# Moving part of the last image's feed-forward evictions from ScalarE to VectorE in a convolution, scan and attention kernel

## The chip, the cores and the metric

The kernel runs on one core of one Trainium2 chip. The metric is the device time of one execution in microseconds (us), of which the median of several runs is taken.

The core has five engines with a queue of their own each. PE (TensorE) multiplies matrices into PSUM, DVE (VectorE) and ACT (ScalarE) work element by element and read PSUM and SBUF, POOL (GpSimd) works element by element on SBUF, and SP (SyncE) issues the transfers (DMAs) between SBUF and the device's main memory. An engine takes its instructions in the order in which the program issued them. Where one needs another engine's result, it waits on a semaphore.

## What is computed

Eight images of 96 channels and 64 x 64 points go through two layers. Layer 0 is a normalization, a projection with a depthwise convolution, a selective scan in four directions, and two further convolutions with a channel gate. Layer 1 is a linear attention (no softmax) and a feed-forward net whose products take e5m2 operands and whose sums are rounded to float16. The part that matters here is the feed-forward net:

```python
q_mul = lambda x: _float_quantize(x, 5, 2)     # e5m2
q_acc = lambda x: _float_quantize(x, 5, 10)    # float16
def _qlinear(x, W, b):
    y = q_acc(jnp.einsum('bsk,nk->bsn', q_mul(x), q_mul(W)))
    return q_acc(y + q_mul(b))
h = jax.nn.relu(_qlinear(x, W1, b1))           # 96 -> 384
y = _qlinear(h, W2, b2)                        # 384 -> 96
...
t = t + _L1_attn_ref(_ln_t(t), ...)
t = t + _L1_ffn_ref(_ln_t(t), ...)
```

So the inner layer's sum is rounded to float16, a bias is added, the result is cut at zero and rounded to float16 again, and then it is rounded to e5m2 as the operand of the second product.

## The kernel before

Data lie with channels on the partitions. The 4096 points of an image are cut into 8 chunks of 512 (`T`), and nearly every instruction works on one chunk. The work of an image has three parts: `front` (normalization, projection, convolution), the scan (the long loop over `units`, line 1092 on), and `back_end` (gate, two convolutions, attention, feed-forward). While the scan of one image runs, the front of the next image and the back end of the one before are issued between the scan's instructions, a step at a time. Only the back end of the last image has no scan to lie beside.

That last back end is issued behind the scan, from line 1152 on. Four sets of tiles, called kits, take the chunks in turn: `kit_b` with the tag f1, and three more with the tags f0, y01 and y2. `side_by_side` runs one stage after the other, and in each stage one stream for each kit. With 8 chunks and 4 kits, each kit does 2 chunks of a stage, so a stage has two rounds. The stages are `first_conv`, `second_conv`, `channel_gate`, `attention`, `joined` and `feed_forward`, the last.

A stream is a Python generator. `drained` (and `tick`) advance a clock by one, and let each stream whose time is due issue its next step, kit after kit: f1, f0, y01, y2. A `yield n` asks to be called again n ticks later. The clock exists only while the program is written: it sets the order of the instructions in each engine's queue, and no time on the chip. With all four streams at the same step, each engine's queue has step k of f1, f0, y01 and y2, and then step k + 1 of the four.

`bank(k.tag, ...)` gives a kit its PSUM bank. For the tags f0, f1, y01 and y2 there is one bank each (`BANKS`), so that a kit's next product can be written only when its last has been read out.

One chunk of `feed_forward` is, by lines:

- 767 to 769: PE multiplies the normalized tokens by the attention's matrix, and DVE adds bias and residue (`scalar_tensor_tensor`) into `t`.
- 773, through `norm` (376 to 384) and `inv_std` (369, 370): PE centres, ACT squares and copies, PE averages the squares, and ACT makes the inverse deviation with Ln and Exp.
- 774: DVE multiplies and writes `x8` in e5m2.
- 776 to 782: for each third `f` of the inner layer, PE multiplies (778), and ACT reads the sum out into the float16 tile `h16` (780) and then adds bias and applies Relu in place (781).
- 783: ACT rounds the whole of `h16`, 128 x 1536, to e5m2 in `h8`.
- 787: PE makes the second product in three matmuls.
- 789, 790: ACT reads it out into `o16` and adds the bias.
- 792: POOL adds it to `t`, and 793 asks for the transfer to the output.

A request that goes through `later` is issued 3 ticks on (`HOLD`). The tokens of the second round are asked for at line 771, in the first round.

Of the kernel before, what the change touches and what calls it, by code (L numbers as in the profile page):

```python
# [12 lines left out]
AF = mybir.ActivationFunctionType  # L13
ALU = mybir.AluOpType
# [29 lines left out]
def kernel(ctx: ExitStack, tc: tile.TileContext, a, out):  # L44
# [8 lines left out]
    nc = tc.nc  # L53
# [9 lines left out]
    def bank(tag, name):  # L63
        return psum.tile([P, T], F32, tag=tag, name=name, bufs=BANKS[tag])
# [48 lines left out]
    def later(dst, src):  # L113

        requests.append((clock[0] + HOLD, dst, src))

    def tick():
        clock[0] += 1
        while requests and requests[0][0] <= clock[0]:
            _, dst, src = requests.pop(0)  # L120
            nc.sync.dma_start(dst, src)  # L121
# [60 lines left out]
    with tc.tile_pool(name="raw", bufs=1) as rp:  # L182
# [10 lines left out]
        def widened(name, shape):  # L193
            t = wp.tile(shape, F32, name=name)
            nc.vector.tensor_copy(t, quantized(name, shape, rp))
            return t
# [3 lines left out]
        b1, b2 = widened("b1", [P, 3]), widened("b2", [C, 1])  # L200
# [81 lines left out]
    def landed(*parts):  # L282
        while clock[0] < max(p.ready for p in parts):
            yield 1
# [25 lines left out]
    def back_kit(pool, tag, extra, other=None, upper=0):  # L310

        k = Kit()
        k.tag, k.solo, k.upper = tag, not extra, upper
        if other is None:
            k.ya, k.za, k.bs, k.r, k.d1, k.s1, k.s2, y, z = (plain(pool, f"{tag}b{i}") for i in range(9))
            k.pad = padded(pool, tag + "pad")
        else:
            k.ya, k.za = (x.t for x in other.x)
            k.bs, k.r, k.d1, k.s1 = other.e
            k.s2, y, z = (other.pre[:, i, :] for i in range(3))  # L320
            k.pad = other.pad
        k.yb, k.zb = Part(y), Part(z[64:P])
        k.ya, k.za, k.bs = Part(k.ya), Part(k.za), Part(k.bs)
        if pool is None:
            return k
        k.t2 = Part(k.r), k.ya
        k.ln = Part(pool.tile([C + 1, T], F32, name=tag + "ln"))
        nc.gpsimd.memset(k.ln.t, 1.0)
        k.im = other.im if other else Part(pool.tile([C + 1, 18, W2], F32, name=tag + "im"))
        k.m3 = [Part(pool.tile([C, 8, W2], F32, name=f"{tag}m3{i}")) for i in range(2)]  # L330
        k.gm = gm0 if not extra else pool.tile([P, 8, W2], F32, name=tag + "gm")
        if extra:
            nc.gpsimd.memset(k.gm, 0.0)
        k.x8 = pool.tile([C, T], F8, name=tag + "x8")
        k.h16 = pool.tile([P, 3, T], F16, name=tag + "h16")
        k.h8 = pool.tile([P, 3, T], F8, name=tag + "h8")
        k.o16 = pool.tile([C, T], F16, name=tag + "o16")
        return k
# [33 lines left out]
    def norm(k, srcs, sq, d):  # L372

        ps = bank(k.tag, "ctr")[:C, :]
        for i, src in enumerate(srcs):
            nc.tensor.matmul(ps, cen_c, src, start=i == 0, stop=i == len(srcs) - 1)  # L376
        yield PA
        nc.scalar.activation(sq, ps, AF.Square)
        nc.scalar.copy(d, ps)  # L379
        yield 1  # L380
        ps = bank(k.tag, "var")[:C, :]
        nc.tensor.matmul(ps, ones_c, sq, start=True, stop=True)  # L382
        yield PA
        inv_std(ps, ps)
        yield 1
        return ps

    place = [None]
    CALM = (0, 1, 8, 9, 16, 17)

# [136 lines left out]
    def back_end(b, s):  # L527
# [212 lines left out]
        def normed_again(k, n, c):  # L740
            fetch(k.ln, lnd[:, bass.ts(c, T)])
            fetch(k.t2[n % 2], x1d[:, bass.ts(c, T)])
# [18 lines left out]
        def feed_forward(k, cs):  # L761

            for n, c in enumerate(cs):
                t = k.t2[n % 2].t[:C]
                yield from landed(k.ln, k.t2[n % 2])
                ps = bank(k.tag, "att")[:C, :]
                nc.tensor.matmul(ps, small["qkvf"], k.ln.t, start=True, stop=True)
                yield PA
                nc.vector.scalar_tensor_tensor(t, ps, bff, t, ALU.add, ALU.add)  # L769
                if n + 1 < len(cs):  # L770
                    normed_again(k, n + 1, cs[n + 1])
                yield 1
                rs = yield from norm(k, (t,), k.s1[:C], k.d1[:C])
                nc.vector.tensor_tensor(k.x8, k.d1[:C], rs, ALU.mult, saturate=False)
                yield 1
                for f in range(3):
                    ps = bank(k.tag, "ff1")
                    nc.tensor.matmul(ps, w1[:, bass.ts(f, P)], k.x8, start=True, stop=True)
                    yield PA
                    nc.scalar.copy(k.h16[:, f, :], ps)  # L780
                    nc.scalar.activation(k.h16[:, f, :], k.h16[:, f, :], AF.Relu, bias=b1[:, f : f + 1])
                    yield 1
                nc.scalar.activation(k.h8, k.h16, AF.Copy, saturate=False)
                yield 1
                ps = bank(k.tag, "ff2")[:C, :]
                for f in range(3):
                    nc.tensor.matmul(ps, w2[:, f, :], k.h8[:, f, :], start=f == 0, stop=f == 2)
                yield PA
                nc.scalar.copy(k.o16, ps)
                nc.scalar.activation(k.o16, k.o16, AF.Identity, bias=b2)  # L790
                yield 2
                nc.gpsimd.tensor_tensor(t, t, k.o16, ALU.add)  # L792
                later(out[b, :, bass.ts(c, T)], t)
                yield 1

        chunks = range(NC)[::-1]
        return (
            (gated, chunks), (first_conv, chunks[1::2]), (second_conv, chunks), (channel_gate, None),
            (attention, chunks), (joined, None), (feed_forward, chunks),
        )  # L800


    def settled():

        yield SETTLE
# [19 lines left out]
    def drained(*streams):  # L825
        while any(s.on for s in streams):
            tick()
            for s in streams:
                s.run()

    def all_issued():
        drained(Stream(iter((HOLD + 1,))))

    def side_by_side(stages, kits):

        for stage, cs in stages:
            todo = [cs] if cs is None else [cs[i :: len(kits)] for i in range(len(kits))]
            drained(*(Stream(stage(k, c)) for k, c in zip(kits, todo)))
            drained(Stream(settled()))
# [312 lines left out]
    with tc.tile_pool(name="end", bufs=1) as pool:  # L1152
        kits = [kit_b, back_kit(pool, "f0", True, kit_f, 1)]
        kits += [back_kit(pool, t, True, None, i) for i, t in enumerate(("y01", "y2"))]
        drained(Stream(settled()))
        side_by_side(final[1:], kits)
        all_issued()

# [66 lines left out]
```

## Time and profile before

| what | us |
|---|---|
| median of 3 runs | 11342.24 |
| lowest and highest of the 3 | 11338.22, 11354.75 |
| the profiled execution's own time | 11372.37 |
| its span in the trace | 11370.7 |
| first ACT instruction of the last `feed_forward`, from the span's start | 11297.59 |
| last DMA of the output issued | 11367.74 |

The profile is that of one execution. Times in the trace count from the span's start. A line of the timeline gives start, duration, engine, line, operation, output and inputs by the program's names, shapes, and in brackets the idle time of the engine ahead of it and what ended it. The names are cut: `f1h`, `f0h`, `y01h` and `y2h` stand for both `h16` and `h8` of the four kits, `f1o` for `o16`, `f1x` for `x8`, `ff` for the PSUM banks. A row of the list of groups gives line, engine, operation, names, shapes and count, then the busy time in us and the mean of one in ns, and then the idle time ahead of it. The table by stretches gives for each engine the busy time in the stretch and, in brackets, the number of instructions.

### The profile page before, as it was taken

To read this page: it belongs to the slowest core of one execution; us is meant where nothing else is said; L and a number is where in the kernel's file an instruction comes from. 1 tells how busy PE (TensorE), PEld (TensorE's weight loads), DVE (VectorE), ACT (ScalarE), POOL (GpSimd) and SP (SyncE) were. 2 spreads that over 40 slices of the span, in tenths; PEclk is the share of its full clock that TensorE was granted. 3 is DMA by queue.
4 is the path that set the end of the run, shared out by engine and by line. 5 is a ranking of instruction groups with operands and counts; after the bars stand their busy time and mean duration, and the time that the engine had idled before them with its cause. 6 is when DMAs were issued, how large, how long until landed. Compare 5 with 4: busy or idle time off the path is not lost. (4 is left out here: it accounts for less than half of the span.)

```text
span 11370.7 us, 97041 instructions
## 1 busy us (share of the span) xinstructions
PE 8567.3 (75%) x23270; PEld 2328.5 (20%) x23270; DVE 10367.4 (91%) x10828; ACT 7508.4 (66%) x14939; POOL 10398.7 (91%) x2783
## 2 busy tenths in 40 slices
PE   6577657887778877888678876788768887676677
PEld 2111112222122211222112221222212221111122
DVE  0799999999999999999999999999999999999991
ACT  3566656767666676667766676666766667666674
POOL 0799999999999999999999999999999999999990
PEclk8678778888788877889778887888878888787787
DMA  2788878898888888888888888889888888888872
GB/s 71 171 197 197 201 189 210 209 225 196 203 210 212 219 198 202 210 215 215 195 207 210 216 214 194 210 205 228 202 200 211 212 220 195 198 198 195 201 188 78
DMA packets 1081039, 2253.24 MB, mean 198 GB/s; under 512 B 419609, under 2 KB 420314, under 8 KB 949395
## 3 DMA queue, kind: packets, MB, share of 16 engines
q1 hardware_dynamic: 1080467, 2247.05, 81.3%
q8 instruction: 184, 3.01, 0.1%
q14 instruction: 388, 3.18, 0.1%
HBM read 1507.14 MB, written 336.69 MB: 162 GB/s over the span
## 5 line engine op out<-in xcount | busy, mean ns | idle before, releaser
L946 POOL TENSOR_TENSOR hb<-b,du 128x2048 f32<-128x2048 f32 x1536 | 6939.0, 4535 | 21.3 <-DMA du<-ua 14.3
L1062 ACT ACTIVATE da<-delta,w_a_logs 128x512 f32<-128x512 f32 x6144 | 4216.7, 689 | 696.3 <-DVE hb L1123 575.8
L972 PE MATMUL p<-hb,halves 128*64 128x512 f32 x12288 | 3822.7, 731 | 800.1 <-POOL hb L952 382.1
L1123 DVE TENSOR_TENSOR_SCAN da<-da,carry,hb 128x512 f32<-128x512 f32 x3087 | 3949.0, 1279 | 58.0 <-ACT da L1062 54.3
L952 POOL TENSOR_TENSOR hb<-hb,c 128x2048 f32<-128x2048 f32 (+2 forms) x768 | 2984.9, 3887 | 304.7 <-ACT carry L1131 252.2
L1123 DVE TENSOR_TENSOR_SCAN hb<-da,carry,hb 128x512 f32<-128x512 f32 x2289 | 2781.0, 1264 | 57.7 <-ACT da L1062 56.7
L1125 DVE TENSOR_TENSOR hb<-da,c 128x512 f32<-128x512 f32 x3528 | 2440.5, 692 | 154.0 <-DVE da L1123 0.9
L1126 ACT COPY carry<-da 128x1 f32<-128x1 f32 x3528 | 554.9, 157 | 2351.6 <-DVE hb L1125 2341.1
L972 PEld LDWEIGHTS p<-hb,halves 128*64 128x64 f32 x12288 | 916.2, 161 | 3540.7 <-issue 2129.5
L434 PE MATMUL conv<-f0im,taps 97*128 97x512 f32 (+1 forms) x2088 | 903.5, 664 | 95.9 <-ACT f0pre L490 54.3
L928 POOL TENSOR_TENSOR ua<-nat,ua 128x512 f32<-128x512 f32 x256 | 327.3, 1279 | 257.5 <-DMA b<-xd 257.5
L1123 DVE TENSOR_TENSOR_SCAN da<-da,hb 128x512 f32<-128x512 f32 x441 | 537.7, 1219 | 26.0 <-POOL hb L946 24.6
L925 DVE SCALAR_TENSOR_TENSOR nat<-dt,nat 128x512 f32<-128x512 f32 x384 | 259.5, 676 | 238.9 <-ACT nat L923 238.9
L911 PE MATMUL dt<-dts,dt_w 7*64 7x512 f32 (+1 forms) x1024 | 450.0, 657 | 16.9 <-DVE nat L925 12.4
L981 PE MATMUL p<-u,ident 128*128 128x512 f32 x768 | 438.3, 699 | 3.6 <-DMA u<-y 3.6
L376 PE MATMUL ctr<-f1b,cen_c 96*96 96x512 f32 x460 | 271.9, 697 | 193.4 <-DVE f1b L769 158.8
L434 PEld LDWEIGHTS conv<-f0im,taps 97*128 97x128 f32 (+1 forms) x2088 | 254.6, 174 | 681.6 <-issue 523.5
L1123 DVE TENSOR_TENSOR_SCAN hb<-da,hb 128x512 f32<-128x512 f32 x327 | 377.9, 1204 | 4.9 <-ACT da L1062 4.9
L382 PE MATMUL var<-f1b,ones_c 96*96 96x512 f32 x346 | 207.4, 684 | 153.6 <-ACT f1b L379 145.3
L792 POOL TENSOR_TENSOR f1b<-f1b,f1o 96x512 f32<-96x512 f32 x58 | 67.7, 1167 | 252.0 <-ACT f1o L790 251.9
L1131 ACT COPY carry<-hb 128x4 f32<-128x4 f32 (+2 forms) x768 | 146.8, 191 | 197.4 <-DVE hb L1123 184.8
L655 PE MATMUL cab<-f1m,cab_w 96*96 96x512 f32 x348 | 206.0, 719 | 90.9 <-ACT f1b L664 41.4
(416 smaller groups left out, 7710.5 us busy)
## 6 DMA issues: line engine op xcount, KB each, us to landing
b<-xd SPq DMA_DIRECT2D x1024, 512.0 KB
c<-xd SPq DMA_DIRECT2D x1024, 512.0 KB
delta<-nat SPq DMA_DIRECT2D x1536, 128.0 KB
du<-ua SPq DMA_DIRECT2D x1024, 128.0 KB
y<-yt SPq DMA_DIRECT2D x512, 256.0 KB
u<-y SPq DMA_DIRECT2D x384, 256.0 KB
ua<-u SPq DMA_DIRECT2D x256, 256.0 KB
du<-ub SPq DMA_DIRECT2D x512, 128.0 KB
```

Of the source, the lines that this page charges most:

```text
L376: nc.tensor.matmul(ps, cen_c, src, start=i == 0, stop=i == len(srcs) - 1)
L434: nc.tensor.matmul(ps, taps[:, t, lo : lo + n], im[:, r0 + dy : r0 + dy + 8, dx : dx + HW], start=t == 0, stop=t == 8,)
L911: nc.tensor.matmul(ps, dt_w[32 * w.k : 32 * w.k + R + 1, d], w.dts, start=True, stop=True)
L928: nc.gpsimd.tensor_tensor(x, u.nat, x, ALU.mult)
L946: nc.gpsimd.tensor_tensor(hb, u.bc[0, g], u.du[j].unsqueeze(1).to_broadcast([P, G, T]), ALU.mult)
L952: nc.gpsimd.tensor_tensor(hb, hb, u.bc[1, TILES[n][0]][:, lo:, :], ALU.mult)
L972: nc.tensor.matmul(ps, halves, u.hb[n][:, i, :], start=TILES[n][0] == 0 and m == 0, stop=False, skip_group_check=True)
L981: nc.tensor.matmul(ps, w, x, start=False, stop=True, skip_group_check=True)
L1062: nc.scalar.activation(da[q], u.delta[j], AF.Exp, scale=a_neg[:, u.k, j, g * G + m : g * G + m + 1])
L1123: nc.vector.tensor_tensor_scan(dd if banked else x, dd, x, 0.0 if u.start else col, ALU.mult, ALU.add)
L1125: nc.vector.tensor_tensor(hb[:, m, :], d, u.bc[1, g][:, m, :], ALU.mult)
L1126: kept.append(lambda col=col, d=d, at=first_at: nc.scalar.copy(col, d[:, at : at + 1]))
```

## The change

A Python flag, `alone`, is false while the scans are issued. It is set true behind the last scan, just ahead of the stages of the last image's back end that follow `gated`. Where it is true, `feed_forward` has VectorE read out thirds 0 and 1 of the inner layer (a `tensor_copy` into float16, and a `tensor_scalar` in place that adds the bias and takes the maximum with 0), while ScalarE keeps third 2. The rounding of all of `h16` to e5m2 goes to VectorE too. The 7 earlier images keep the old code.

```diff
+    alone = [False]
     place = [None]
...
                     ps = bank(k.tag, "ff1")
                     nc.tensor.matmul(ps, w1[:, bass.ts(f, P)], k.x8, start=True, stop=True)
                     yield PA
-                    nc.scalar.copy(k.h16[:, f, :], ps)
-                    nc.scalar.activation(k.h16[:, f, :], k.h16[:, f, :], AF.Relu, bias=b1[:, f : f + 1])
+                    if alone[0] and f < 2:
+                        nc.vector.tensor_copy(k.h16[:, f, :], ps)
+                        nc.vector.tensor_scalar(
+                            k.h16[:, f, :], k.h16[:, f, :], b1[:, f : f + 1], 0.0, ALU.add, ALU.max
+                        )
+                    else:
+                        nc.scalar.copy(k.h16[:, f, :], ps)
+                        nc.scalar.activation(k.h16[:, f, :], k.h16[:, f, :], AF.Relu, bias=b1[:, f : f + 1])
                     yield 1
-                nc.scalar.activation(k.h8, k.h16, AF.Copy, saturate=False)
+                if alone[0]:
+                    nc.vector.tensor_copy(k.h8, k.h16, saturate=False)
+                else:
+                    nc.scalar.activation(k.h8, k.h16, AF.Copy, saturate=False)
                 yield 1
...
         drained(Stream(settled()))
+        alone[0] = True
         side_by_side(final[1:], kits)
         all_issued()
```

## The prediction

> **What bounds the kernel now.** I read the page first, then the stretches of its end, then the timelines of ACT, DVE and PE there. The page gives the frame:
>
> ```profile
> span 11370.7 us, 97041 instructions
> PE 8567.3 (75%) x23270; PEld 2328.5 (20%) x23270; DVE 10367.4 (91%) x10828; ACT 7508.4 (66%) x14939; POOL 10398.7 (91%) x2783
> ```
>
> DVE and POOL fill the span as long as scans run. The last scan instruction ends near 11090, and what follows is short. The changed code runs only there: the last `feed_forward` begins at 11289.56 (line 767), so the change can touch some 81 of 11371 us, 0.7%. The table by stretches for its first round:
>
> ```profile
> 11297.59:11306.18 8.59, 6.98 (x17) 2.34 (x16) 2.05 (x3) 8.46 (x16) 0.00 (x0) 1.00 0.16 49
> 11306.18:11320.91 14.73, 5.16 (x10) 1.03 (x9) 0.68 (x1) 14.34 (x25) 0.00 (x0) 0.52 0.00 0
> 11320.91:11326.40 5.49, 3.97 (x9) 1.68 (x9) 0.00 (x0) 5.49 (x5) 0.00 (x0) 0.50 0.00 0
> ```
>
> The columns are PE, PEld, DVE, ACT, POOL. The second row is the read-out and Relu of the inner layer, the third the cast to e5m2. ACT is busy throughout both, and DVE does next to nothing. So in this stage, unlike in the rest, ACT sets the end. Its timeline gives the pitch:
>
> ```profile
> 11306.18 0.58 ACT L780 CAST f1h<-ff 128x512 f16<-128x512 f32 x1
> 11306.80 0.72 ACT L781 ACTIVATE f1h<-f1h,b 128x512 f16<-128x512 f16 x1
> 11307.42 0.57 ACT L780 CAST f0h<-ff 128x512 f16<-128x512 f32 x1
> ...
> 11320.91 1.47 ACT L783 ACTIVATE f1h<-f1h 128x1536 fp8e5<-128x1536 f16 x1
> 11322.29 1.47 ACT L783 ACTIVATE f0h<-f0h 128x1536 fp8e5<-128x1536 f16 x1
> ...
> 11326.40 0.56 ACT L789 CAST f1o<-ff 96x512 f16<-96x512 f32 x1
> ```
>
> One pair (780, 781) takes (11320.91 - 11306.18) / 12 = 1.227 us, one cast 1.37. From 11306.18 to 11326.40 ACT does 12 pairs and 4 casts, and then 4 pairs for the outer layer up to 11331.39. The second round has the same steps 35.1 us later (11341.28 to 11361.50). Between the rounds, ACT waits 1.29 us for line 376, which follows the last read-out of `o16` (line 789 of y2 at 11330.07) through the PE products of lines 767 and 376. That wait moves along with the read-out.
>
> [...] the two PSUM copies of line 211 below differ by 99 ns for 96 elements, 1.03 ns each. No row shows a 16-bit operation on DVE[...]. The e5m2 casts of line 190 below differ by 58 ns for 96 elements, 0.60 ns each[...]. POOL has four 1.15 us additions at each round's end, after the casts.
>
> ```profile
> L211 DVE COPY cab_w<-fold 97x288 f32<-97x288 f32 x1 | 0.5, 457 | 1.4 <-PE fold L210 1.4
> L211 DVE COPY wx<-fold 97x192 f32<-97x192 f32 x1 | 0.4, 358 | 1.0 <-PE fold L210 1.0
> L190 DVE CAST q_w<-raw_w 96x384 fp8e5<-96x384 f32 x1 | 0.4, 356 | 4.4 <-DMA raw_w<-in_w_dram 4.4
> L190 DVE CAST q_w<-raw_w 128x288 fp8e5<-128x288 f32 x1 | 0.3, 298 | 0.0
> L234 DVE TENSOR_SCALAR dd_a<-ident,sum_ds 128x128 f32<-128x128 f32 x1 | 0.3, 286 | 0.0
> L234 DVE TENSOR_SCALAR dd_b<-ident,sum_ds 64x64 f32<-64x64 f32 x1 | 0.2, 245 | 0.0
> ```
>
> **The prices on DVE.**
> - Copy of 512 from PSUM: 358 + 320 x 1.03 = 0.69 us (row L774, a 96x512 product with one operand in PSUM, is 0.68).
> - Bias and maximum, 512 of float16 in place: rows L234 leave about 0.20 fixed for a tensor_scalar with a [P, 1] operand. [...] I take 0.34.
> - Cast of 1536 to e5m2: 356 + 1152 x 0.60 = 1.05 by the slope of L190[...]. I take 1.0.
> - Pitch. Of the scan loop:
>
> ```profile
> 5000.30 1.28 DVE L1123 TENSOR_TENSOR_SCAN da<-da,carry,hb 128x512 f32<-128x512 f32 x1
> 5001.61 0.69 DVE L1125 TENSOR_TENSOR hb<-da,c 128x512 f32<-128x512 f32 x1
> 5002.22 1.28 DVE L1123 TENSOR_TENSOR_SCAN da<-da,carry,hb 128x512 f32<-128x512 f32 x1
> ```
>
> Line 1125 reads what the scan wrote and starts 0.03 behind it; the next scan reads nothing of 1125 and starts 0.08 before its end. So a pair (copy, then in place) advances DVE by 0.69 + 0.03 + 0.34 - 0.08 = 0.98 us, and a cast by 0.92.
>
> **The change, part by part, in one round.**
>
> Removed from ACT: 8 pairs, 8 x 1.227 = 9.8 us, and 4 casts, 5.5 us. If nothing else came late, 15.3 us a round. It doesn't all come back, since DVE's part stands in series with what remains.
>
> *Thirds 0 on DVE.* In DVE's queue they stand behind the four products of line 774, whose last the timeline has here:
>
> ```profile
> 11306.29 0.68 DVE L774 TENSOR_TENSOR y2x<-y2b,var 96x512 fp8e5<-96x512 f32 x1 [0.49 <-ACT var L370]
> ```
>
> The first copy can start at 11306.29 + 0.68 - 0.08 = 11306.89, 0.7 later than ACT's did. That is the wait which the move adds; behind it on DVE stands only feed-forward work. Four pairs end at 11306.89 + 3.92 = 11310.81.
>
> *Thirds 1 on DVE.* Each kit has one bank, so its product for third 1 starts when its first copy is done; three other kits' pairs (2.9 us) cover that. The copy for f1 ends at 11311.50.
>
> *Thirds 2 on ACT.* PE starts f1's product 0.06 later (as line 774's end at 11303.45 to line 778 at 11303.51). It lasts 0.38 to 0.6, and ACT starts about 0.1 behind that: 11312.1. DVE frees the next kit's bank each 0.98, faster than ACT's 1.227, so ACT goes on at its own pitch: 4 x 1.227 = 4.9, to 11317.0.
>
> *Casts on DVE.* Thirds 1 end at 11310.81 + 3.92 = 11314.73; f1's third 2 has been done since about 11313.5. Its cast ends at 11315.7. PE's three matmuls take 0.8 to 1.4 (line 787), and the read-out can start between 11316.7 and 11317.4. I take 11317.2, level with the end of ACT's thirds 2. The other casts follow at 0.92, under ACT's pitch, so lie hidden; without that cover each adds its excess.
>
> *Sum.* Line 789 of f1 moves from 11326.40 to 11317.2: 9.2 us. The four outer pairs and all behind them move along, POOL's additions and the output's DMAs on SP too; they depend on ACT's read-outs alone. The additions start when the casts are over[...]. The second round gains the same: 18.4 us in all.
>
> Against the profiled execution (span 11370.7, and 1.7 around it, 11372.4): 11354.0. The runs' median lies 30.1 below that execution, a difference I carry unchanged: 11342.2 - 18.4 = 11323.8.
>
> [...]
>
> **The rivals.**
> - [...] (chance 0.18). Gains of 4.1 to 6.2 a round, so 11330 to 11334. For it: no row shows float16 on DVE[...]. Against it: L190 and L234 both beat 1.03 ns an element.
> - *The whole relief of ACT* (0.07). If DVE's part were hidden, 15.3 a round: 11311.6. Against it: thirds 1 and 2 must wait for the banks, and ACT has nothing else to do while DVE works through thirds 0.
> - *DVE becomes the bound* (0.03, slower). The place is the float16 pair: if the in-place step waited for the copy's data to be written far longer than 0.03. The last read-out starts about 1.3 after the last cast, so it decides from 8 pairs + 4 casts above 11330.07 - 1.3 - 11306.89 = 21.9 us. With casts at 1.68 a pair must pass 1.9 us; at 2.1 each round loses 1.6: 11345.5. Against it: the scan loop's dependent pairs wait 0.03, and line 774 writes e5m2 at the speed of float32 (line 718, 0.68 both).
> - *The change not doing what it says*: the flag is true before the generators of the last stages are run, so all 8 chunks take the new branch. No chance given.
>
> **How the numbers follow.** The forecast's case has 0.72, with 16.8 to 19 us gained: 11323 to 11325.5 before noise. The three runs spread over 16.5 us, so I add about 7 either way: 11316 to 11332[...]. The limit of 0.2%, about what a measurement of this kernel can tell from no change, is 22.7 us, thus 11319.6. The forecast's case passes it by the runs' spread alone, with 0.3 (0.22 of all), the whole-relief case nearly always (0.07): faster 0.29. Slower by 0.2% needs 11364.9, which no case gives but by spread: 0.01. Within: 0.70.
>
> **What would show it.** In the new trace, line 789 of f1 about 10.3 us behind the first DVE copy (11306.89 to 11317.2); a pair on DVE every 0.98; 8 pairs and 4 casts less on ACT in each round; ACT idle about 5.9 us between line 370 and its thirds 2. [...] A first ACT third well before 11312 would mean I misread the banks. A change ahead of 11300 would mean that something outside this sum counts.

## The result, and the profile after

Over 20 runs of each, the changed kernel takes 11334.58 us (11324.17 to 11340.0) and the kernel before 11352.42 us (11335.86 to 11363.4). The ratio is 0.9985, with a 95% interval of 0.9978 to 0.9991: 17.8 us less, 0.16%. The forecast was 18.4 us less. But it stood on a kernel before at 11342.24, and so said 11323.8, with a range up to 11333 (11332 from the forecast's own case, 11333 with the rival of the slower DVE counted in). The gain was foreseen, and the time wasn't.

The page of the changed kernel:

```profile
span 11333.8 us, 97039 instructions
PE 8544.5 (75%) x23270; PEld 2320.9 (20%) x23270; DVE 10390.3 (92%) x10868; ACT 7478.7 (66%) x14899; POOL 10398.8 (92%) x2783
```

ACT has 40 instructions less, DVE 40 more: 16 pairs and 8 casts, as the diff says. The span is 36.9 us shorter than that of the profile before. That is not the change's gain; the sections below take the two apart.

The stretches of the first round of the last `feed_forward` (columns as before: PE, PEld, DVE, ACT, POOL, then granted clock, DMA share, GB/s):

```profile
11278.18:11286.85 8.67, 7.04 (x17) 2.34 (x16) 2.05 (x3) 8.54 (x16) 0.00 (x0) 1.00 0.46 137
11286.85:11297.87 11.02, 6.32 (x13) 1.72 (x13) 10.70 (x20) 4.89 (x9) 0.00 (x0) 0.59 0.00 1
11297.87:11304.82 6.95, 6.95 (x20) 3.04 (x19) 4.07 (x6) 4.93 (x9) 4.61 (x4) 0.91 0.29 85
```

The inner layer took 20.22 us of ACT (14.73 + 5.49); now it takes 11.02, and the engine that fills them is DVE, with 10.70 busy. In the last row a third engine has taken over: PE is busy for 6.95 of 6.95 us.

ACT's timeline shows the wait that the move adds, and the pace from round to round:

```profile
11286.28 0.57 ACT L370 ACTIVATE var<-var 96x512 f32<-96x512 f32 x1
11292.80 0.59 ACT L787 CAST f1h<-ff 128x512 f16<-128x512 f32 x1 [5.94 <-PE ff L779]
...
11297.87 0.58 ACT L799 CAST f1o<-ff 96x512 f16<-96x512 f32 x1
...
11304.82 0.59 ACT L378 ACTIVATE f1b<-ctr 96x512 f32<-96x512 f32 x1 [1.89 <-PE ctr L376]
```

ACT stands idle for 5.94 us until DVE has freed the bank for f1's third 2. The outer read-out (now line 799) starts 0.06 behind the end of ACT's thirds (11297.09 + 0.72), where an operation of ACT in this row otherwise starts 0.10 before the end of the one ahead of it. So it waits some 0.15 us for PE's product, which ends at 11297.84. From the round's first ACT of line 378 (11278.18) to the read-out it takes 19.69 us; before, 28.81 (11297.59 to 11326.40).

DVE's timeline has the prices:

```profile
11286.89 0.68 DVE L775 TENSOR_TENSOR y2x<-y2b,var 96x512 fp8e5<-96x512 f32 x1 [0.49 <-ACT var L370]
11287.49 0.68 DVE L782 CAST f1h<-ff 128x512 f16<-128x512 f32 x1
11288.21 0.35 DVE L783 TENSOR_SCALAR f1h<-f1h,b 128x512 f16<-128x512 f16 x1
11288.48 0.68 DVE L782 CAST f0h<-ff 128x512 f16<-128x512 f32 x1
...
11295.39 0.95 DVE L791 CAST f1h<-f1h 128x1536 fp8e5<-128x1536 f16 x1
11296.26 0.95 DVE L791 CAST f0h<-f0h 128x1536 fp8e5<-128x1536 f16 x1
```

The first copy does wait for the last product of line 775. A pair takes 0.99 us from copy to copy, a cast 0.87 from start to start.

### The profile page after: what moved, and what is told of

It is laid out like the page before. It is cut to its first block, busy times and chain, and to the rows that moved or that the text cites. A ratio compares the mean times of both kernels' runs of the same rounds, so it can differ in the third digit from the quotient of the medians.

```text
span 11333.8 us, 97039 instructions
## 1 busy us (share of the span) xinstructions
PE 8544.5 (75%) x23270; PEld 2320.9 (20%) x23270; DVE 10390.3 (92%) x10868; ACT 7478.7 (66%) x14899; POOL 10398.8 (92%) x2783
## 5 line engine op out<-in xcount | busy, mean ns | idle before, releaser
L619 PE MATMUL cab<-f1im,cab_w 97*32 97x512 f32 x1044 | 264.7, 627 | 12.8 <-DMA f1im<-xld 7.9
```

## The experiments

Most of the kernels below were run once, and a single total time can't be used: runs of the kernel before lay anywhere from 11324 to 11379 us. So each trace is measured from the first ACT instruction of line 378 in the last `feed_forward`. All of the change lies behind it, and that part repeats: the kernel before took 73.1 us to the end of the span in two traces (11370.7 - 11297.59 and 11355.2 - 11282.08), the changed kernel 55.6 in two (11333.8 - 11278.18 and 11325.3 - 11269.69).

The theory: the outer read-out comes when the later of two chains is done. One is ACT's four thirds, which start behind five DVE copies. The other is DVE's eight pairs, first cast and PE's product. The rivals: the gain is a common share of the work taken from ACT, or it is held back by ACT's wait for the banks.

| kernel | first read-out | next round's line 378 | end of span |
|---|---|---|---|
| before | 28.81 | 35.09 | 73.1 |
| e1_same | 28.81 | 35.09 | 73.1 |
| e2_evict | 25.04 | 31.32 | 65.5 |
| e3_cast | 23.32 | 29.69 | 62.2 |
| changed | 19.69 | 26.64 | 55.6 |
| e4_extra | 22.32 | 29.71 | 61.3 |
| e5_late | 20.95 | 28.94 | 59.2 |
| e6_split | 17.19 | 24.16 | 50.5 |
| e7_spare | 19.69 | 26.65 | 55.6 |
| e8_both | 17.20 | 24.17 | 50.7 |
| e9_again | 19.69 | 26.66 | 55.6 |

All columns are us behind the first ACT of line 378.

**e1_same.** The kernel before, with no edit.

> The kernel before, unchanged, timed against itself. If the level of the kernel lies near the 11352 of the twenty runs and single runs scatter by some 10 us, the ratio is 1.000 within 0.001, and a median of few runs can lie 5 to 10 us off. If instead 11342, the median of three runs in the forecast, is the level of the kernel, the medians are at 11342 or below. Its profile should have the last feed-forward round as before (28.8 us from the first ACT of line 378 to the read-out of the outer layer, line 789), while the start of that round moves by several us from execution to execution.

Measured: 11347.23 us (13 runs, 11327.9 to 11363.93) beside 11350.19 (17 runs) of the same kernel; ratio 0.9997, 0.9989 to 1.0005. Its round is that of the first trace:

```profile
11282.08 0.59 ACT L378 ACTIVATE f1b<-ctr 96x512 f32<-96x512 f32 x1 [14.42 <-PE ctr L376]
...
11310.89 0.56 ACT L789 CAST f1o<-ff 96x512 f16<-96x512 f32 x1
```

The round takes the same 28.81 us, but begins 15.5 us sooner. So the scatter is ahead of the changed code. Both medians lie above the 11342 of the forecast: three runs didn't fix the level of this kernel.

**e2_evict.** Thirds 0 and 1 on DVE, the casts on ACT.

```diff
-                if alone[0]:
-                    nc.vector.tensor_copy(k.h8, k.h16, saturate=False)
-                else:
-                    nc.scalar.activation(k.h8, k.h16, AF.Copy, saturate=False)
+                nc.scalar.activation(k.h8, k.h16, AF.Copy, saturate=False)
```

> Only thirds 0 and 1 on VectorE, the casts to e5m2 back on ScalarE. Series theory (the outer read-out comes when the later is done of ScalarE's four thirds behind five VectorE copies, and of VectorE's eight pairs, first cast and product): thirds 2 end as in the changed kernel, 19.6 us behind the round's first ACT of line 378, and four casts of 1.37 us follow in series: the read-out at 25.1 us, a gain of 3.7 us a round. Rival (the gain is the work taken from ScalarE times a common share, 9.1/15.3 = 0.6): 9.8 us taken gives 5.8 us, the read-out at 23.0 us.

Measured: 25.04 us. One run, 11346.73 us.

```profile
11279.53 0.59 ACT L378 ACTIVATE f1b<-ctr 96x512 f32<-96x512 f32 x1 [10.23 <-PE ctr L376]
...
11299.08 1.47 ACT L790 ACTIVATE f1h<-f1h 128x1536 fp8e5<-128x1536 f16 x1
...
11304.57 0.56 ACT L796 CAST f1o<-ff 96x512 f16<-96x512 f32 x1
```

9.8 us of pairs taken from ACT brought 3.8. The other 6 us are ACT's wait of 5.95 for the banks.

**e3_cast.** The casts on DVE, all thirds on ACT.

```diff
-                    if alone[0] and f < 2:
-                        nc.vector.tensor_copy(k.h16[:, f, :], ps)
...
+                    nc.scalar.copy(k.h16[:, f, :], ps)
+                    nc.scalar.activation(k.h16[:, f, :], k.h16[:, f, :], AF.Relu, bias=b1[:, f : f + 1])
```

> Only the casts to e5m2 on VectorE, all thirds on ScalarE. Series theory: the twelve pairs of ScalarE end 23.3 us behind the round's first ACT of line 378, and the casts lie beside the last of them, so the outer read-out comes at 23.3 us, a gain of the full 5.5 us a round. Rival (a common share of 0.6 of the work taken): 3.3 us, the read-out at 25.5 us.

Measured: 23.32 us. One run, 11321.64 us.

```profile
11257.75 0.59 ACT L378 ACTIVATE f1b<-ctr 96x512 f32<-96x512 f32 x1 [11.38 <-PE ctr L376]
...
11281.07 0.56 ACT L793 CAST f1o<-ff 96x512 f16<-96x512 f32 x1
```

The 5.49 us of casts come back in full: the smaller half of the work taken is the larger half of the gain. A common share of 0.6 falls with these two.

**e4_extra.** One more maximum with 0 behind each DVE pair.

```diff
+                        nc.vector.tensor_scalar(k.h16[:, f, :], k.h16[:, f, :], 0.0, None, ALU.max)
```

> The changed kernel with one more maximum with 0 in place on VectorE behind each of its pairs (it changes no value). The pair grows by 0.27 to 0.3 us. Series theory with VectorE's own chain as the later one (eight pairs, cast, product): the outer read-out moves from 19.7 to about 21.9 us behind the first ACT of line 378, 2.2 us a round. With ScalarE's thirds as the later one: four added operations ahead of its start, 1.1 us. If VectorE's work lay hidden beside ScalarE's: 0.

Measured: 22.32 us, 2.63 more. One run, 11341.24 us. DVE's timeline, then ACT's:

```profile
11287.47 0.68 DVE L782 CAST f1h<-ff 128x512 f16<-128x512 f32 x1
11288.19 0.35 DVE L783 TENSOR_SCALAR f1h<-f1h,b 128x512 f16<-128x512 f16 x1
11288.57 0.29 DVE L786 TENSOR_SCALAR f1h<-f1h 128x512 f16<-128x512 f16 x1
11288.78 0.68 DVE L782 CAST f0h<-ff 128x512 f16<-128x512 f32 x1
```

```profile
11294.09 0.58 ACT L788 CAST f1h<-ff 128x512 f16<-128x512 f32 x1 [7.25 <-PE ff L779]
...
11300.48 0.58 ACT L800 CAST f1o<-ff 96x512 f16<-96x512 f32 x1 [1.10 <-PE ff L798]
```

A pair grew by 0.32 (11288.78 - 11287.47 is 1.31), a little more than the 0.27 to 0.3 that I had set. ACT's thirds start 1.31 later (7.25 in place of 5.94), and then ACT waits again, 1.10 for PE's product. The shift is that of eight operations, 2.6: DVE's chain is the later one as soon as it grows. In the changed kernel the two end nearly together.

**e5_late.** ACT takes third 0 in place of third 2.

```diff
-                    if alone[0] and f < 2:
+                    if alone[0] and f > 0:
```

> The changed kernel with another third on ScalarE: third 0, and thirds 1 and 2 on VectorE. ScalarE then starts at once (8.6 us behind the round's first ACT of line 378, no idle time of 5.9 us), but VectorE's third 1 of each kit follows ScalarE's pitch of 1.23 us, and its eight pairs stand behind one another: a model of the queues gives the outer read-out at 21.0 us, 1.3 us later than the changed kernel's 19.7. If the idle time of ScalarE were what costs, the read-out would come up to 5 us earlier.

Measured: 20.95 us. One run, 11340.78 us.

```profile
11279.90 0.59 ACT L378 ACTIVATE f1b<-ctr 96x512 f32<-96x512 f32 x1 [10.24 <-PE ctr L376]
...
11288.49 0.58 ACT L787 CAST f1h<-ff 128x512 f16<-128x512 f32 x1
...
11300.85 0.58 ACT L799 CAST f1o<-ff 96x512 f16<-96x512 f32 x1 [7.34 <-PE ff L797]
```

ACT starts at once, the 5.9 us of idle time are gone from there, and 7.34 stand ahead of the outer read-out. The read-out comes 1.3 us later than in the changed kernel, at the 21.0 that the model gave, so ACT's idle time is not what costs.

**e7_spare.** The changed kernel with third 2 issued second and in a bank of its own.

```diff
-                for f in range(3):
-                    ps = bank(k.tag, "ff1")
+                for f in (0, 2, 1) if alone[0] else range(3):
+                    spare = {"f1": "dt"}.get(k.tag, "da")
+                    ps = bank(spare if alone[0] and f == 2 else k.tag, "ff1")
```

> The changed kernel with third 2 of each kit issued second and put in one of the PSUM banks that the scans have left free (tags da and dt), so that ScalarE need not wait for VectorE's read-outs. Series theory with VectorE's chain binding too: ScalarE's idle time of 5.9 us ahead of its thirds falls below 1 us and its thirds end 14 us behind the round's first ACT of line 378, but eight pairs, the first cast and the product on VectorE and PE still put the outer read-out at 19.4 us (19.7 in the changed kernel). Rival (the wait for the banks is what keeps the relief from coming back): up to 5 us earlier, 14.7 us.

Measured: 19.69 us, the changed kernel's figure. One run, 11325.24 us.

```profile
11267.90 0.59 ACT L378 ACTIVATE f1b<-ctr 96x512 f32<-96x512 f32 x1 [11.27 <-PE ctr L376]
...
11277.97 0.58 ACT L788 CAST f1h<-ff 128x512 f16<-128x512 f32 x1 [1.40 <-PE ff L780]
...
11287.59 0.58 ACT L800 CAST f1o<-ff 96x512 f16<-96x512 f32 x1 [4.60 <-PE ff L798]
```

ACT's wait ahead of its thirds is down from 5.94 to 1.40. I had said below 1; PE's products of third 0 stand ahead in PE's queue. Now 4.60 us come ahead of the read-out. So the wait for banks was not what kept the relief: DVE's chain alone gives the same end. (The run changes the bank and the order of the thirds together.)

**e6_split.** The work shared by kit, on both engines at once.

```diff
+    SHARED = ((0, "f1"), (2, "f1"), (1, "f0"), (2, "f0"), (0, "y2"))
+    OUTER = ("y01", "y2")
...
-                    if alone[0] and f < 2:
+                    if alone[0] and (f, k.tag) in SHARED:
...
+                if alone[0] and k.tag in OUTER:
+                    nc.vector.tensor_copy(k.o16, ps)
+                    nc.vector.tensor_scalar(k.o16, k.o16, b2, None, ALU.add)
+                else:
...
+                adder = nc.vector if alone[0] and k.tag in OUTER else nc.gpsimd
+                adder.tensor_tensor(t, t, k.o16, ALU.add)
```

> The work of the last image's feed-forward shared by kit instead of by third: 5 of 12 pairs of the inner layer on VectorE (f1 thirds 0 and 2, f0 thirds 1 and 2, y2 third 0), the casts on VectorE, and the outer read-out, bias and addition of y01 and y2 on VectorE. A model of the queues, which gives the changed kernel's 19.6 us, gives 17.3 us from the first ACT of line 378 to the first outer read-out, 23.7 us in place of 26.6 to the next round, and the last addition done at 22 us in place of 26.0: about 6.6 us less than the changed kernel, 24 us less than the kernel before, ratio 0.9979. If PE, which works without a break from the first cast to the next round's centring in the changed kernel, sets the pace between the rounds, the first round gains less than 1 us and the whole some 4 us.

Measured: 17.19 us to the first read-out, 24.16 to the next round, and 50.5 to the end, 5.1 less than the changed kernel. Over 22 runs 11334.37 us beside 11354.4 of the kernel before: ratio 0.9983, 0.9976 to 0.9991.

```profile
11316.71 0.56 ACT L805 CAST f1o<-ff 96x512 f16<-96x512 f32 x1
...
11323.68 0.59 ACT L378 ACTIVATE f1b<-ctr 96x512 f32<-96x512 f32 x1 [4.43 <-PE ctr L376]
```

The first part went as modelled. The first round gains 2.5 us (26.64 to 24.16), so the rival in which PE sets the pace and leaves less than 1 us falls there. 0.5 us were lost between the rounds (24.16 for 23.7), where ACT now waits 4.43 for PE's centring, and 1.3 at the end. Of these 1.3, POOL's and DVE's timelines show 0.7:

```profile
11343.49 1.15 POOL L809 TENSOR_TENSOR f0x<-f0x,f0o 96x512 f32<-96x512 f32 x1
11343.74 1.05 DVE L803 TENSOR_SCALAR y01o<-y01o,b 96x512 f16<-96x512 f16 x1
11345.42 0.35 DVE L803 TENSOR_SCALAR y2o<-y2o,b 96x512 f16<-96x512 f16 x1
```

DVE's bias of y01 takes 1.05 us beside an addition of POOL, and that of y2 takes 0.35 when POOL is done. In this trace the three such operations that met an addition took 0.58 to 1.05 us and ended 0.14 to 0.15 behind its end, and the one that met none took 0.35. The runs can't tell this version from the changed kernel (0.9983 and 0.9985); only the trace does.

**e8_both.** The same, and DVE adds up two terms for PE in the attention stage.

```diff
+                if alone[0]:
+                    nc.vector.tensor_tensor(x1, x1, bs, ALU.add)
+                    terms = ((dgate, t), (dskip2, x1))
+                else:
+                    terms = ((dgate, t), (dskip2, x1), (dskip2, bs))
```

> The work shared by kit as in the run before, and VectorE adds two of the three terms of the attention stage's sum ahead of PE, so that PE makes two products a chunk (dgate by t, dskip2 by x1 + base) in place of three; the sum's order changes in rounding. In the attention's two rounds PE sets the pace: four products of 0.86 us less in each, 3.4 us, 6.9 us in all. With the 23 us of the sharing by kit: 29 us less than the kernel before, ratio 0.9974. If PE doesn't bind there, 23 us and 0.998.

Measured over 8 runs: 11317.94 us (11306.16 to 11323.86) beside 11345.74; ratio 0.9974, 0.9963 to 0.9984, as expected. The two rounds of the attention now begin at

```profile
11212.03 0.59 ACT L378 ACTIVATE f1b<-ctr 96x512 f32<-96x512 f32 x1 [0.28 <-PE ctr L376]
11232.94 0.59 ACT L378 ACTIVATE f1b<-ctr 96x512 f32<-96x512 f32 x1 [0.28 <-PE ctr L376]
```

These are 20.9 us apart. The same stretch takes 26.7 in e9_again, on the same chip (11220.80 to 11247.53), and 24.0 to 26.9 over all ten traces that keep the three products, so it varies by nearly as much as the 3.4 us of four products. From the scans to the last `feed_forward` e8_both takes 162.4 us, beside 171.2 in e9_again and 172.8 in e7_spare: 9 to 10 less, where 6.9 were expected. What else differs there was not separated. Its median is the lowest here, but its interval overlaps that of the changed kernel below.

**e9_again.** The changed kernel once more, no edit.

> The changed kernel once more, timed on the same chip beside the two above: 17.5 us in the last two rounds, ratio 0.9985 within its interval. If its true gain were that of the forecast's case without the loss between the rounds, 18.4 us, the ratio would be 0.9984, which the runs can't tell apart; the trace can, by 26.6 us from round to round (25.9 without the loss).

Measured over 20 runs: 11328.94 us beside 11345.74; ratio 0.9986, 0.9979 to 0.9993. The medians of both kernels lie some 6 us below those of the first measurement, and their ratio stayed. By the record, e7, e8 and e9 ran on another chip (8) than e1 to e6 (0), each beside the kernel before on its own chip; whether the lower level is the chip's, the runs don't show. Its rounds are 26.66 us apart, so the loss between the rounds is there again.

## Why the prediction was right or wrong, by its own steps

*Where the time goes.* Right: everything gained lies behind the first ACT of line 378 in the last `feed_forward`, 73.1 to 55.6 us, 17.5.

*The prices on DVE.* Right. Copy 0.68 (0.69 set down), bias and maximum 0.35 (0.34), cast 0.95 (1.0), pair 0.99 (0.98). The 0.34 was my estimate, since no row of the profile before has float16 on DVE; it came out right. The 0.20 that rows L234 leave as fixed, with the 1.03 ns an element of line 211, would have made 0.73. With the same 0.20, the 0.35 is 0.29 ns an element. DVE's casts and POOL's additions didn't meet: the last cast ends at 11298.95, and POOL's first addition starts at 11299.28. With these prices, the rival with the chance of 0.18 falls, in which DVE takes 1.03 ns an element for bias and maximum, or for the casts too (one each 1.68 us), and the gain is 4.1 to 6.2 us a round; so does the one in which DVE's pairs pass 1.9 us.

*Thirds 1 and 2.* Right. ACT's thirds begin 14.62 us behind line 378 (11292.80 - 11278.18), against 14.5 in the prediction (11312.1 - 11297.59), its idle time is 5.94 against 5.9, and the read-out comes at 19.69 against 19.6. 9.1 us a round, against 9.2.

*The reason why not all of ACT's relief comes back.* Half right. I named the wait for the banks and DVE's series together. e7_spare takes the first away and nothing changes, e4_extra stretches the second and the end moves by all of it. Either alone suffices: ACT's thirds behind the banks end at 19.55 us in e2_evict (11299.08 - 11279.53), and DVE's chain gives 19.69 in e7_spare. The two end nearly level, as the prediction had it (11317.0 against 11316.7 to 11317.4).

*"That wait moves along with the read-out."* Wrong by 0.67 us. From the first outer read-out to the next round's line 378 it took 6.28 us and now takes 6.95. Before, PE and ACT had:

```profile
11330.69 1.10 PE L767 MATMUL att<-y2ln,qkvf 97*96 97x512 f32 x2
11332.68 0.59 ACT L378 ACTIVATE f1b<-ctr 96x512 f32<-96x512 f32 x1 [1.29 <-PE ctr L376]
```

PE's timeline of the changed kernel has the reason:

```profile
11296.40 1.44 PE L797 MATMUL ff<-f1h,q_w 128*96 128x512 fp8e5 x3 [0.68 <-DVE f1h L791]
...
11299.67 0.81 PE L797 MATMUL ff<-y2h,q_w 128*96 128x512 fp8e5 x3
11300.32 1.02 PE L768 MATMUL att<-f1ln,qkvf 97*96 97x512 f32 x2
...
11303.76 1.02 PE L376 MATMUL ctr<-f1b,cen_c 96*96 96x512 f32 x2
```

Before, ACT's read-outs (1.22 us each) set the pace of line 767: y2's product at 11330.69 follows y2's read-out, which ends at 11330.63. Now the casts come each 0.87, and PE works without a break worth naming from the first cast's end to the centring: 12 second products, 8 attention matmuls, then line 376. What is late next behind ACT and DVE is PE, and the prediction didn't ask for that. There is one such passage, so 9.1 + 9.1 - 0.7 gives the 17.5.

*"The runs' median lies 30.1 below that execution, a difference I carry unchanged: 11342.2 - 18.4 = 11323.8."* This is the step that failed. The 11342.2 was a median of three. Twenty runs, these three among them, put it at 11352.42, 10.2 us higher, so that the profiled execution lay 20.0 above the level and not 30.1; 11352.4 - 18.4 is 11334.0, and 11334.58 was measured. The allowance for noise failed with it: about 7 us either way, drawn from three runs, was put about a level that itself could be 10 us off. In the later measurements the level was 11350.19 and 11354.4, and 11345.74 on the other chip (for the first measurement the record names no chip). Two of the three runs are among the three lowest of the twenty. That can be bad luck; whether anything but chance set these three low, no run shows.

Where does the scatter come from? Taking the two profiles apart: of the 36.9 us between their spans, 17.5 are the change. 0.7 lie ahead of a mark just behind the scans (the clearing of `gram`, line 676 and now 677, at 11106.04 and 11105.35). The remaining 18.7 lie in the last image's convolutions and attention, which the change doesn't touch. This stretch, from that clearing to the first ACT of line 378, in the kernel before, the changed one and e2_evict:

```profile
11106.04:11297.59 191.55, 148.73 (x449) 59.00 (x450) 24.67 (x47) 57.21 (x93) 0.17 (x2) 0.78 0.34 98
```

```profile
11105.35:11278.18 172.83, 131.50 (x449) 54.59 (x450) 24.68 (x47) 57.21 (x92) 0.17 (x2) 0.87 0.36 104
```

```profile
11110.46:11279.53 169.07, 127.26 (x447) 49.89 (x446) 24.67 (x47) 57.20 (x92) 0.17 (x2) 0.89 0.37 107
```

DVE and ACT are busy for the same time in each. PE is not: its busy time is 17.2 us less in the second than in the first, of the 18.7, and the granted clock (0.78, 0.87, 0.89) goes with the length. PE is the busiest engine of this stretch, and its clock differs from execution to execution. e6_split's profile, with 0.78, took 186.5. The first slices of 10 us show how, in the profile before and then in that of the changed kernel (the clock is the third number from the end):

```profile
11105.00:11115.00 10.00, 7.94 (x8) 1.57 (x8) 0.94 (x2) 1.47 (x3) 1.22 (x4) 0.50 0.44 124
11115.00:11125.00 10.00, 8.95 (x13) 3.19 (x14) 1.37 (x3) 2.89 (x5) 0.00 (x0) 0.63 0.18 53
```

```profile
11105.00:11115.00 10.00, 8.11 (x17) 2.62 (x18) 0.90 (x2) 2.53 (x5) 0.53 (x2) 1.00 0.54 159
11115.00:11125.00 10.00, 6.85 (x14) 1.44 (x12) 2.37 (x4) 3.58 (x6) 0.00 (x0) 1.00 0.07 21
```

The same stage begins at half the clock in one execution (0.50) and at the full one in the other (1.00). PE was busy for much the same share in both first slices, 7.94 and 8.11 of 10 us. What sets the granted clock of an execution, no run here shows. Over the ten traces whose code is the same up to here (all but e8_both) this stretch varies by 22 us (169.1 to 191.6), and the mark behind the scans by 30 (11083.25 in e3_cast to 11113.06 in e6_split), while single runs of the kernel before vary by 55. Over whole runs the mean clock and the time go together in the two later measurements on chip 0 (correlations of -0.84 over 17 runs of the kernel before, and -0.83 over 27) and less in that on chip 8 (-0.40 over 27), whose runs spread over 14 us. What moves the mark stays open, and so does the 10.2 us of the level.

## What to carry to other kernels

An engine's relief comes back only as far as the next chain allows: add up the series that the work joins on its new engine, and then ask which engine the earlier end will make late, PE here. When a forecast is a small difference on a long time, its error is that of the level it is hung on; state the difference, and give the level the width that its few runs have. Where runs scatter more than the effect, measure the trace from a mark just ahead of the changed code: there the same kernel repeats within 0.1 us (73.1 twice, 55.6 twice), while its whole time moves by more than 10 (11335.86 to 11363.4 over the twenty runs of the kernel before).

## What the runs showed of the hardware that I had not expected

- A tensor_scalar on 512 float16 elements takes 0.35 us on DVE with a [P, 1] operand, both with two operations (line 783) and with one (line 803 of e6_split), and 0.29 with a constant and one operation (line 786 of e4_extra). The difference is 0.06.
- The same tensor_scalar took 0.58 to 1.05 us beside an addition of POOL (line 803 of e6_split), and a read-out from PSUM beside one took 0.70 (line 802 of e6_split at 11318.07).
- The e5m2 cast of 1536 float16 elements takes 0.95 us on DVE and 1.47 on ACT.
- Over the same instructions, the granted PE clock of a 169 to 192 us stretch lay between 0.78 and 0.89 in eight traces (before, changed, e1 to e6), while the mean over each whole run lay within 0.821 to 0.830.
